# Smaller and re-timed projection pieces in a gated cross-attention and mixture-of-experts kernel, with a re-ordered start and a moved last result

## The chip, the cores and the metric

The kernel runs on one core of a Trainium2 chip. It is one launch: its inputs lie in the chip's memory, its output goes there. The metric is the device time in microseconds (us), here the median of three executions. All times and rows in this document come from those executions, from one further execution recorded by the hardware profiler, or from questions put to that record's trace.

## What is computed

Four batches of 512 tokens of width 256 attend to a context of 1601 keys of width 192, in 16 heads of 16; then a mixture of experts with a shared expert and the best two of eight follows. All of it is in float32. The reference, cut to what matters:

```python
def xattn(x, y):                       # x (4,512,256), y = ctx (4,1601,192)
    q = heads(x @ Wq + bq); k = heads(y @ Wk + bk); v = heads(y @ Wv + bv)
    attn = softmax(q @ k.T * 0.25)     # 16 heads of 16
    h = relu((attn @ v) @ W1 + b1)     # 256 -> 512
    return h @ W2 + b2                 # 512 -> 256

def moe(x):                            # 8 routed experts, 2 per token, I = 512
    probs = sigmoid(x @ Wr + rb)
    w, idx = top_k(probs, 2)
    return expert_shared(x) + sum(w[k] * expert[idx[k]](x) for k in range(2))
    # expert(x) = (silu(x @ Wg.T) * (x @ Wu.T)) @ Wd.T

x = x + tanh(g_xattn) * xattn(layernorm(x), ctx)
x = x + tanh(g_ffn) * moe(layernorm(x))
```

## The kernel before

**Groups and steps.** The 16 heads of a batch are worked on in four groups of four, so there are 16 groups over the four batches. A group has 13 steps, one for each tile of 128 keys (the last has 65). In a step TensorE makes the four scores of the next key tile (L475), ScalarE takes their exponentials (L484), TensorE adds the values of the present tile to the group's sums (L496, `add_values`), and for the softmax's shift TensorE makes scores once more for the *next* group (L416), of which VectorE takes row maxima (L427). The work of a step comes in two bursts of two scores and two maxima each. Scores have three PSUM banks, maxima three, the values' sums one, and one bank ("ms", `side()`) serves everything else. A step is written (g, k) within a batch or over all groups: group g from 0 to 15, key tile k from 0 to 12; group 4b is the first of batch b. So groups 0 to 3 are batch 0, and 12 to 15 the last batch.

**The hand-written order.** Inside the first part of the program the order on TensorE, ScalarE, VectorE and SyncE (SP, which issues DMAs) is that of the code. Work besides attention is cut into pieces and written into a list `late` of each step (`put`, `put_all`, L628 and L635): they are issued behind the step's bursts. The pieces are these:

- `make_k` (L359): a part of K for two groups: 2 matmuls of 401 columns and a ScalarE eviction into `kd`; four parts (`chunks`) make 1601 columns. `spread` (L376) then copies a group's rows out of `kd` into one of three key buffers, by four DMAs.
- `make_q` (L332): half of the Q of two groups, 2 matmuls of 256 columns and an eviction into `qd`; `spread_q` (L350) copies a group's rows by four DMAs.
- `make_v` (L387): V of one key tile, 2 matmuls of 256 columns. `make_xnT` (L305): half of the transposed layer norm, 4 transposes of 128 columns.
- `mlp_in` (L559, 2 matmuls of 256 columns, 8 pieces a batch) and `mlp_out` (L574, 4 matmuls of 128 columns, 8 pieces) for the batch before; `residual` (L589), which is VectorE work after every second `mlp_out`; then `rstd_of` (L261) and `apply` (L284) make the second layer norm, with GpSimd (Pool) taking the last of it; `route` (L594) sends its rows to memory and makes the router's logits.
- `divide`, `collect`, `normalize`: the division of the sums by the softmax's denominator, and the DMAs ahead of it.

A step with a piece that uses TensorE is put into the set `large`. A step that isn't large, is not its group's first and still has maxima to make splits `add_values` into two halves of 256 columns, one behind each burst; all others add the values in one go behind the first burst:

```python
        halves = maxima and s > 0 and s % NKT and s not in large
```

**Where the pieces stand.** While batch b is attended to, K and Q for its own second pair of groups stand in (4b, 0) to (4b, 5) (K only for b > 0; batch 0's is made at the start), and those for the first pair of the next batch in (4b+2, 0) to (4b+2, 7): K in quarters, then xnT in two, then Q in two. V of the next batch fills group 4b+3. The previous batch's `mlp_in` stand in (4b, 7) to (4b+1, 2), its `mlp_out` in (4b+1, 3) to (4b+1, 10), and `rstd_of` and `apply` in (4b+1, 11). Steps without any TensorE piece are called free steps below.

**The start.** `first_loads` (L199) issues the first DMAs. ScalarE's queue issues the one of wk, into `wk_slots`, then those of bk (two), bq, the gates and bv; SP's issues x of batch 0 in two halves, the context in four parts (two, then wq, then two), and wv. ScalarE then copies the weights of K out of `wk_slots` without their gaps (L737), K's first two parts are made (`first_k`), ScalarE and SP issue the first `spread` between them (L380, two DMAs each), ScalarE copies xnT (L303), and the first Q, the rest of K and the maxima of group 0 follow.

**The experts.** Behind attention the 4096 pairs of token and expert are sorted into tiles of 128 rows of one expert each. 35 tiles (`SURE`) are always run, four more stand in a branch that is taken only if the sorting needs them (`tc.If(n_used[0] > SURE)`, L1226); in the profiled execution it isn't taken. `run_tiles` (L1170) makes a tile's hidden layer `hT2[i]`; `give` (L1143) multiplies it by the expert's down weights, VectorE scales the result (`y`, three buffers) and Pool sends it to memory by an indirect DMA (`rows_y`). `give(SURE - 1)` stands ahead of the branch. Behind it the results are loaded (L1243), added to x (L1256) and stored, with pieces of the shared expert (`fill`, L804 and L827) between them.

Of the kernel before, what the change touches and what calls it, by code (L numbers as in the profile page):

```python
# [8 lines left out]
FP = mybir.dt.float32  # L9
# [5 lines left out]
P = 128  # L15
# [11 lines left out]
def kernel(  # L27
# [45 lines left out]
    nc = tc.nc  # L73
    B, D, M = ctxT.shape
    NT, H = x.shape
    S = NT // B
# [27 lines left out]
        xb = resid.tile([P, NTB, H], FP, name=f"xb{b}")  # L104
        xs.append(xb)

    def load_x(b, parts=1):
        n = NTB // parts
        for k in range(parts):
# [72 lines left out]
    def load_ctx(b, parts=((0, M),)):  # L182
        for o, n in parts:
            nc.sync.dma_start(
                out=ctx_t[:KC, :, o : o + n],
                in_=ctxT[b].rearrange("(c p) m -> p c m", p=KC)[:, :, o : o + n],
            )

    wk_slots = p1.tile([P, NF, S], FP, tag="hid", name="wk_slots")[:KC, :2, :]

    def without_gaps(dst, src, queue):
# [7 lines left out]
    def first_loads():  # L199

        nc.scalar.dma_start(out=wk_slots, in_=wk.rearrange("(c p) n -> p c n", p=KC))
        load_x(0, 2)
        load_ctx(0, chunks[:2])
        nc.sync.dma_start(out=wq_t, in_=wq.rearrange("(c p) n -> p c n", p=P))
        load_ctx(0, chunks[2:])
        without_gaps(bk_d, bk, nc.scalar)
        nc.scalar.dma_start(out=bq_t, in_=bq)
        nc.scalar.dma_start(out=gt, in_=gates.partition_broadcast(P))
        nc.scalar.dma_start(
            out=wv_t[KC : KC + 1, 1, :], in_=bv.rearrange("(o n) -> o n", o=1)  # L210
        )
        nc.sync.dma_start(out=wv_t[:KC], in_=wv.rearrange("(c p) n -> p c n", p=KC))

    def other_loads():
# [95 lines left out]
    def half_of(h):  # L310

        return slice(0, S) if h is None else slice(h * S // 2, (h + 1) * S // 2)
# [16 lines left out]
            )  # L329
        nc.scalar.activation(qT[i], ps, AF.Identity, bias=bq_t[:, i : i + 1])  # L330

    def make_q(b, h2, h):  # L332

        ps = side()
        n = half_of(h)
        for c in range(2):
            nc.tensor.matmul(
                ps[:, n],
                lhsT=wq_d[:, c, h2 * P : (h2 + 1) * P],
                rhs=xnT[b][:, c, n],  # L340
                start=(c == 0),
                stop=(c == 1),
            )
        if not h:
            qd[b, h2] = sp1.tile([P, S], FP, tag="qd", name=f"qd_{b}_{h2}")
        nc.scalar.activation(
            qd[b, h2][:, n], ps[:, n], AF.Identity, bias=bq_d[:, h2 : h2 + 1]
        )
# [7 lines left out]
                out=qT[i][j * HS : j * HS + HD, :], in_=qd[b, g // 2][r : r + HD, :]  # L356
            )

    def make_k(b, h2, part, ps=None):  # L359
        if part == 0:  # L360
            kd[b, h2] = sp1.tile([P, M], FP, tag="kd", bufs=2, name=f"kd_{b}_{h2}")
        o, n = chunks[part]
        ps = side() if ps is None else ps
        for c in range(2):
            nc.tensor.matmul(
                ps[:, :n],
                lhsT=wk_t[:, c, h2 * P : (h2 + 1) * P],
                rhs=ctx_t[:KC, c, o : o + n],
                start=(c == 0),
                stop=(c == 1),  # L370
            )
        nc.scalar.activation(
            kd[b, h2][:, o : o + n], ps[:, :n], AF.Identity, bias=bk_d[:, h2 : h2 + 1]
        )
# [264 lines left out]
    for b in range(B):  # L639
        i = b * G  # L640
        nb = b + 1 if b + 1 < B else None
        for g in range(G):
            if i + g:
                put(late, i + g, *((1, normalize) if i + g == NG - 1 else (0, collect)), i + g - 1)

        if b:
            put_all(i, range(NCH), [(make_k, b, 1, part) for part in range(NCH)])
            put(late, i, NCH - 1, spread, i + 2)
            put_all(i, range(2, 2 + LOTS), [(divide, b - 1, 1, t) for t in range(LOTS)])
        put_all(i, (4, 5), [(make_q, b, 1, h) for h in range(2)])  # L650
        put(late, i, 5, spread_q, i + 2)
        put(late, i + 1, 0, spread, i + 3)
        put(late, i + 1, 2, spread_q, i + 3)
        if b:
            mlp = [(mlp_in, b - 1, n % NF, n // NF) for n in range(2 * NF)]
            put_all(i, (7, 8, 9, 10, 12), mlp[: NF + 1])
            put_all(i + 1, (0, 1, 2), mlp[NF + 1 :])
            for n in range(2 * NTB):
                put(late, i + 1, 3 + n, mlp_out, b - 1, n // 2, n % 2)
                if n % 2:  # L660
                    put(late, i + 1, 4 + n, residual, b - 1, n // 2)
            put(late, i + 1, 11, rstd_of, b - 1, mv2, rstd2, nc.gpsimd)
            put(late, i + 1, 11, apply, b - 1, mv2, rstd2, nc.gpsimd)
            put_all(i + 2, (8, 9, 10, 12), [(route, b - 1, n) for n in range(4)])

        put_all(i + 2, range(2, 2 + LOTS), [(divide, b, 0, t) for t in range(LOTS)])
        if nb:
            put(late, i, 4, load_ctx, nb)
            for t in range(NTB):
                put(late, i, 6 + t, stats1, nb, t)  # L670
            put(late, i + 1, 3, rstd_of, nb, mv1, rstd1, nc.gpsimd)
            put(late, i + 1, 3, apply, nb, mv1, rstd1, nc.gpsimd)
            if not b:
                put(late, i + 1, 8, load_expert, 0, w_sh)
            put_all(i + 2, range(NCH), [(make_k, nb, 0, part) for part in range(NCH)])
            put(late, i + 2, NCH - 1, spread, i + 4)
            put_all(i + 2, (4, 5), [(make_xnT, nb, c) for c in range(2)])
            put_all(i + 2, (6, 7), [(make_q, nb, 0, h) for h in range(2)])
            put(late, i + 2, 7, spread_q, i + 4)
            put(late, i + 3, 0, spread, i + 5)  # L680
            put(late, i + 3, 2, spread_q, i + 5)
            vals = [(make_v, nb, kt) for kt in range(NKT)]
            put_all(i + 1, (12,), vals[:1])
            put_all(i + 3, [kt for kt in range(NKT) if kt != NKT - 2], vals[1:])
# [38 lines left out]
    with tc.manual_schedule(  # L723
# [12 lines left out]
        for c in range(2):  # L736
            nc.scalar.copy(  # L737
                wk_t[:, c, :].rearrange("p (h d) -> p h d", d=HD),
                wk_slots[:, c, :].rearrange("p (h d) -> p h d", d=HS)[:, :, :HD],
            )  # L740
        for t in range(NTB):
            stats1(0, t)
        rstd_of(0, mv1, rstd1, nc.vector)
# [426 lines left out]
    def run_tiles(first, end):  # L1170
        for i in range(first, end):
            own(i)
            gp = ps_g.tile([P, I], FP, tag="g", name="gp")
            half(i, gp, 0)
            up = ps_u.tile([P, I], FP, tag="u", name="up")
            half(i, up, 2)
            sg = work.tile([P, I], FP, tag="sg")
            nc.scalar.activation(sg, gp, AF.Silu)  # L1178
            hT2[i] = work.tile([P, I], FP, tag="hT2", name=f"hT2_{i}")
            nc.vector.tensor_tensor(hT2[i], sg, up, ALU.mult)  # L1180
            if i + 1 < end:
# [15 lines left out]
    with tc.manual_schedule(engines=every):  # L1197
        choose()
        fill(3)
        finding = find_places()  # L1200
        next(finding)
        fill(2)
        next(finding)
        ready = [prepare(0)]
        for _ in finding:
            pass
        fill(4)
        for part in range(NJ // PART):
# [12 lines left out]
        take(0)  # L1221
        fill(1)
        run_tiles(0, SURE)
        fill(1)
        give(SURE - 1)
    with tc.If(n_used[0] > SURE):  # L1226
        with tc.manual_schedule(engines=every):
            take(SURE)
# [4 lines left out]
    with tc.manual_schedule(  # L1233
        engines={mybir.EngineType.PE, mybir.EngineType.DVE, mybir.EngineType.Pool}
    ):
        yk = {}
        for b in range(B):
            for k in range(TOP):
# [120 lines left out]
```

## Time and profile before

| what | value |
|---|---|
| three executions | 1199.41, 1199.28, 1199.27 us |
| median | 1199.28 us |
| profiled execution, its own time | 1199.35 us |
| profiled execution, span of the record | 1197.6 us |
| mean granted clock of TensorE | 0.999 |
| maxima on VectorE, L427 | 744 times, 686 ns each |
| exponentials on ScalarE, L484 | 804 times, 594 ns each |
| DMA queue q1 (loads, spreads, stores) | 43.67 MB |
| DMA queue q0 (indirect transfers) | 8.42 MB |

The span runs from the first to the last recorded instruction; the profiled execution's own time is 1.75 us longer. By the starts of the exponentials the attention steps begin at 58.88 us with (0, 0); ahead of that lie the loads, the first K, Q and maxima, and the first V.

How to read the rows: `PE` is TensorE's matmuls and `PEld` its weight loads, which overlap them; `DVE` is VectorE, `ACT` ScalarE, `POOL` GpSimd; a name with q (`ACTq`) is the engine's sequencer, which issues DMAs and waits on semaphores. In a timeline a row gives the start, the busy time, the engine, the line of the kernel, the instruction, its output and inputs by name (`out<-in`), partitions by elements, and the count of equal neighbours; brackets at its end give the idle time ahead of it and what ended that. In a table of windows a row gives a stretch, its length, and then the busy time of PE, PEld, DVE, ACT and Pool in it with the number of their instructions, the granted clock, the DMA engines' busy share and GB/s. In a row that comes from the page's 40 slices or from the DMA view, each digit is the busy share of one slice in tenths.

### The profile page before, as it was taken

Reading aid. Unit: us, or ns where it says so; the run is one execution under the profiler, and the core shown is the slowest. Engines: PE = TensorE matmul, PEld = TensorE weight load, DVE = VectorE, ACT = ScalarE, POOL = GpSimd, SP = SyncE. Lnnn points to the kernel's source line nnn. Section 1 sums busy time; section 2 is a strip of 40 time slices with the busy share of each in tenths; the row PEclk is TensorE's granted clock in tenths of the full one; section 3 lists DMA queues with packets and bytes.
Section 4 is the critical chain, followed back from the end, with each engine's and each line's share of the span. In section 5 each row is a group of like instructions: output and inputs, shape, how many; then the busy total and the mean of one; then the engine's idle time right before and its main releaser. Section 6 shows DMA issues by size and latency. Waiting matters only on the chain. (4 is left out here: it accounts for less than half of the span.)

```text
span 1197.6 us, 21547 instructions
## 1 busy us (share of the span) xinstructions
PE 1188.0 (99%) x8454; PEld 590.5 (49%) x8454; DVE 738.1 (62%) x1394; ACT 604.6 (50%) x1112; POOL 166.0 (14%) x240
## 2 busy tenths in 40 slices
PE   9999999999999999999999999999999999999998
PEld 3433334333344343343434333343436679999995
DVE  6867767667776765676767667677604843333335
ACT  2265656555655655555556556655682233333330
POOL 2000200000022000002010000002000035555550
PEclk9999999999999999999999999999999999999999
DMA  5311110102100110121011101100009101111106
GB/s 131 107 47 26 56 24 5 28 10 60 27 2 10 37 28 1 22 49 27 2 22 32 19 10 19 28 1 28 1 7 375 58 28 41 52 44 46 46 30 215
DMA packets 37608, 54.00 MB, mean 45 GB/s; under 512 B 9339, under 2 KB 25597, under 8 KB 37506
## 3 DMA queue, kind: packets, MB, share of 16 engines
q1 hardware_dynamic: 32024, 43.67, 13.8%
q0 software_dynamic: 4656, 8.42, 2.3%
q8 instruction: 69, 1.13, 0.4%
q10 hardware_dynamic: 826, 0.50, 0.2%
q14 instruction: 33, 0.27, 0.1%
HBM read 32.88 MB, written 8.80 MB: 35 GB/s over the span
## 5 line engine op out<-in xcount | busy, mean ns | idle before, releaser
L427 DVE TENSOR_REDUCE mxs<-mx 128x1 f32<-128x512 f32 x744 | 479.9, 686 | 214.0 <-PE mx L416 207.2
L484 ACT ACTIVATE es<-sc 128x512 f32<-128x512 f32 x804 | 437.8, 594 | 328.5 <-PE mx L416 274.8
L416 PE MATMUL mx<-ks,qs 32*128 32x512 f32 (+1 forms) x1984 | 481.3, 549 | 0.2 <-DVE mxs L427 0.2
L475 PE MATMUL sc<-qA,ks 32*128 32x512 f32 x1608 | 466.1, 637 | 0.8 <-DVE qA L470 0.8
L475 PEld LDWEIGHTS sc<-qA,ks 32*128 32x128 f32 x1608 | 130.6, 179 | 215.5 <-issue 162.6
L496 PE MATMUL av<-es,vs 128*32 128x512 f32 (+3 forms) x2032 | 232.3, 527 | 0.2
L416 PEld LDWEIGHTS mx<-ks,qs 32*128 32x128 f32 x1984 | 165.3, 183 | 4.3 <-DVE mxs L427 2.4
L496 PEld LDWEIGHTS av<-es,vs 128*32 128x32 f32 (+1 forms) x2032 | 40.4, 108 | 181.3 <-issue 175.6
L269 POOL TENSOR_SCALAR var<-var 128x4 f32<-128x4 f32 x6 | 1.4, 236 | 766.4 <-DVE first L266 766.4
L1180 DVE TENSOR_TENSOR hT<-sg,up 128x512 f32<-128x512 f32 x35 | 24.1, 688 | 111.0 <-PE up L1135 107.7
L1135 PEld LDWEIGHTS gp<-xT,held 128*128 128x128 f32 x560 | 68.0, 192 | 2.2 <-ACT sg L820 0.2
L1135 PE MATMUL up<-xT,held 128*128 128x128 f32 x560 | 68.2, 275 | 0.0
L1135 PE MATMUL gp<-xT,held 128*128 128x128 f32 x560 | 68.2, 275 | 0.0
L1146 PE MATMUL y_ps<-w_all,hT 128*128 x280 | 66.2, 379 | 0.0
L1135 PEld LDWEIGHTS up<-xT,held 128*128 128x128 f32 x560 | 65.3, 192 | 0.0
L393 PE MATMUL ms<-wv_t,ctx_t 96*128 96x256 f32 (+1 forms) x208 | 58.7, 404 | 0.1
L393 PEld LDWEIGHTS ms<-wv_t,ctx_t 96*128 96x128 f32 (+1 forms) x208 | 34.5, 185 | 40.0 <-issue 31.9
L1146 PEld LDWEIGHTS y_ps<-w_all,hT 128*128 128x128 f32 x280 | 50.5, 190 | 5.5
L1178 ACT ACTIVATE sg<-gp 128x512 f32<-128x512 f32 x35 | 20.9, 597 | 61.8 <-PE gp L1135 57.5
L1126 ACT COPY held<-w_all 128x1024 f32 x39 | 40.6, 1046 | 16.0 <-issue 7.1
L1155 POOL DMA_INDIRECT rows_y<-y,dest x35 | 36.2, 1034 | 72.8 <-DVE y L1154 70.3
L1091 POOL DMA_INDIRECT xg<-rows_x,token x38 | 39.2, 1032 | 50.4 <-DVE hits L1079 39.1
(191 smaller groups left out, 954.8 us busy)
## 6 DMA issues: line engine op xcount, KB each, us to landing
ks<-kd SPq DMA_DIRECT2D x60, 100.1 KB, 3.4
w_all<-in_wgT SPq DMA_DIRECT2D x8, 512.0 KB, 10.4
w_all<-in_wuT SPq DMA_DIRECT2D x8, 512.0 KB, 10.2
w_all<-in_wdT SPq DMA_DIRECT2D x8, 512.0 KB, 10.4
w_all<-rows_y SPq DMA_DIRECT2D x8, 512.0 KB, 7.6
ctx_t<-in_ctxT SPq DMA_DIRECT2D x3, 1200.8 KB
rows_x<-xn SPq DMA_DIRECT2D x4, 512.0 KB, 3.0
qs<-qd SPq DMA_DIRECT2D x56, 32.0 KB, 2.0
```

The lines of the kernel that those rows point to most:

```text
L393: nc.tensor.matmul(ps[:n, : NH * HD], lhsT=ctx_t[r, c, o : o + n], rhs=heads[r, c, :, :HD], start=(c == 0), stop=(c == 1),)
L416: nc.tensor.matmul(ps[:, n * REST : (n + 1) * REST] if last else ps, lhsT=qT[i][slot_of(j), qb * P : (qb + 1) * P], rhs=ks[i % 3][slot_of( ...
L427: nc.vector.tensor_reduce(mxs[i][:, qb, j, c : c + 1], ps, AX.X, ALU.max)
L475: nc.tensor.matmul(ps[:n, :], lhsT=ks[i % 3][r, o : o + n], rhs=qA[i][r, :], start=True, stop=True)
L484: nc.scalar.activation(es[(i * NKT + kt) % 2, j][:n], ps[:n], AF.Exp, scale=SCALE)
L496: nc.tensor.matmul(av[i][j * HS : (j + 1) * HS, cols], lhsT=v_of(b, kt)[:n, g * HPG + j, :], rhs=es[(i * NKT + kt) % 2, j][:n, cols], star ...
L1091: nc.gpsimd.indirect_dma_start(out=xg[i % 4], out_offset=None, in_=rows_x, in_offset=bass.IndirectOffsetOnAxis(ap=token[:, i : i + 1], axi ...
L1126: (nc.scalar.copy if engine is nc.scalar else nc.vector.tensor_copy)(held[i % 2].rearrange("p c i -> p (c i)")[:, o * I : (o + 2) * I], w_ ...
L1135: nc.tensor.matmul(ps[:, f * P : (f + 1) * P], lhsT=held[i % 2][:, off + c, f * P : (f + 1) * P], rhs=xT[i][:, c, :], start=(c == 0), stop ...
L1146: nc.tensor.matmul(ps, lhsT=hT2[i][:, f * P : (f + 1) * P], rhs=w_flat[:, bass.ds(owners[i] + 4 * I + f * H, H)], start=(f == 0), stop=(f ...
L1155: ins = nc.gpsimd.indirect_dma_start(out=rows_y, out_offset=bass.IndirectOffsetOnAxis(ap=dest[:, i : i + 1], axis=0), in_=y, in_offset=Non ...
L1180: nc.vector.tensor_tensor(hT2[i], sg, up, ALU.mult)
```

## The change

It has four parts.

1. **K and Q of batch 0's successor.** K for the first pair of batch 1 is made in eighths (201 columns) instead of quarters, in (1, 0) to (1, 7) instead of (2, 0) to (2, 3); xnT goes to (1, 8) and (1, 9), and Q is made in quarters (128 columns) in (2, 4) to (2, 7). The two spreads stay where they were.
2. **The last batch.** K for its second pair is made in eighths in (12, 0) to (12, 7), with its spread behind the last; the two halves of Q go from (12, 4), (12, 5) to (12, 8), (12, 9), and their spread with them. `mlp_in` of the batch before takes (12, 10), (12, 12) and (13, 0) to (13, 5); `mlp_out` takes (13, 6) to (13, 10), (13, 12), (14, 0) and (14, 1); each `residual` follows a step behind; `rstd_of` and `apply` go from (13, 11) to (14, 2).
3. **The start.** ScalarE gets one small copy right behind the issue of wk's DMA, which brings its table load there. The first part of the context is issued between the two halves of x, and the second behind them. The DMAs of the gates and bv are issued behind the copies of K's weights.
4. **The branch.** `give(SURE - 1)` moves behind the branch, and the last sure tile's hidden layer is kept in a part of `x2T` that is free by then, instead of a rotating buffer.

Batches 1 and 2 keep their order. The diff, cut to its core:

```diff
     def first_loads():
         nc.scalar.dma_start(out=wk_slots, in_=wk.rearrange("(c p) n -> p c n", p=KC))
-        load_x(0, 2)
-        load_ctx(0, chunks[:2])
+        nc.scalar.copy(early, ident[:, :1])
+        load_x(0, 2, (0,))
+        load_ctx(0, chunks[:1])
+        load_x(0, 2, (1,))
+        load_ctx(0, chunks[1:2])
         nc.sync.dma_start(out=wq_t, in_=wq.rearrange("(c p) n -> p c n", p=P))
         load_ctx(0, chunks[2:])
         without_gaps(bk_d, bk, nc.scalar)
         nc.scalar.dma_start(out=bq_t, in_=bq)
-        nc.scalar.dma_start(out=gt, in_=gates.partition_broadcast(P))
-        nc.scalar.dma_start(
-            out=wv_t[KC : KC + 1, 1, :], in_=bv.rearrange("(o n) -> o n", o=1)
-        )
         nc.sync.dma_start(out=wv_t[:KC], in_=wv.rearrange("(c p) n -> p c n", p=KC))
...
-    def make_q(b, h2, h):
+    def make_q(b, h2, h, of=2):
-        n = half_of(h)
+        n = slice(h * S // of, (h + 1) * S // of)
...
+    eighths = [(c * (CH // 2 + 1), min(CH // 2 + 1, M - c * (CH // 2 + 1))) for c in range(2 * NCH)]
...
-    def make_k(b, h2, part, ps=None):
+    def make_k(b, h2, part, ps=None, pieces=chunks):
-        o, n = chunks[part]
+        o, n = pieces[part]
...
-        if b:
+        if nb and b:
             put_all(i, range(NCH), [(make_k, b, 1, part) for part in range(NCH)])
             put(late, i, NCH - 1, spread, i + 2)
+        elif b:
+            pieces = [(make_k, b, 1, part, None, eighths) for part in range(2 * NCH)]
+            put_all(i, range(2 * NCH), pieces)
+            put(late, i, 2 * NCH - 1, spread, i + 2)
...
-        put_all(i, (4, 5), [(make_q, b, 1, h) for h in range(2)])
-        put(late, i, 5, spread_q, i + 2)
+        q_at = (4, 5) if nb else (8, 9)
+        put_all(i, q_at, [(make_q, b, 1, h) for h in range(2)])
+        put(late, i, q_at[1], spread_q, i + 2)
...
-            mlp = [(mlp_in, b - 1, n % NF, n // NF) for n in range(2 * NF)]
-            put_all(i, (7, 8, 9, 10, 12), mlp[: NF + 1])
-            put_all(i + 1, (0, 1, 2), mlp[NF + 1 :])
+            free = [(i, kt) for kt in ((7, 8, 9, 10, 12) if nb else (10, 12))]
+            free += [(i + 1, kt) for kt in range(NKT) if kt != NKT - 2 and (kt != NKT - 1 or not nb)]
+            free += [(i + 2, kt) for kt in range(3)]
+            free = iter(free)
+            for n in range(2 * NF):
+                put(late, *next(free), mlp_in, b - 1, n % NF, n // NF)
             for n in range(2 * NTB):
-                put(late, i + 1, 3 + n, mlp_out, b - 1, n // 2, n % 2)
+                at, kt = next(free)
+                put(late, at, kt, mlp_out, b - 1, n // 2, n % 2)
                 if n % 2:
-                    put(late, i + 1, 4 + n, residual, b - 1, n // 2)
-            put(late, i + 1, 11, rstd_of, b - 1, mv2, rstd2, nc.gpsimd)
-            put(late, i + 1, 11, apply, b - 1, mv2, rstd2, nc.gpsimd)
+                    put(late, *divmod(at * NKT + kt + 1, NKT), residual, b - 1, n // 2)
+            at = (i + 1, NKT - 2) if nb else (i + 2, 2)
+            put(late, *at, rstd_of, b - 1, mv2, rstd2, nc.gpsimd)
+            put(late, *at, apply, b - 1, mv2, rstd2, nc.gpsimd)
...
-            put_all(i + 2, range(NCH), [(make_k, nb, 0, part) for part in range(NCH)])
-            put_all(i + 2, (4, 5), [(make_xnT, nb, c) for c in range(2)])
-            put_all(i + 2, (6, 7), [(make_q, nb, 0, h) for h in range(2)])
+            if b:
+                put_all(i + 2, range(NCH), [(make_k, nb, 0, part) for part in range(NCH)])
+                put_all(i + 2, (4, 5), [(make_xnT, nb, c) for c in range(2)])
+                put_all(i + 2, (6, 7), [(make_q, nb, 0, h) for h in range(2)])
+            else:
+                pieces = [(make_k, nb, 0, part, None, eighths) for part in range(2 * NCH)]
+                put_all(i + 1, range(2 * NCH), pieces)
+                put_all(i + 1, (8, 9), [(make_xnT, nb, c) for c in range(2)])
+                put_all(i + 2, (4, 5, 6, 7), [(make_q, nb, 0, h, 4) for h in range(4)])
...
                 wk_slots[:, c, :].rearrange("p (h d) -> p h d", d=HS)[:, :, :HD],
             )
+        nc.scalar.dma_start(out=gt, in_=gates.partition_broadcast(P))
+        nc.scalar.dma_start(
+            out=wv_t[KC : KC + 1, 1, :], in_=bv.rearrange("(o n) -> o n", o=1)
+        )
...
-            hT2[i] = work.tile([P, I], FP, tag="hT2", name=f"hT2_{i}")
+            if i == SURE - 1:
+                hT2[i] = x2T[:, 0, :I]
+            else:
+                hT2[i] = work.tile([P, I], FP, tag="hT2", name=f"hT2_{i}")
...
         fill(1)
-        give(SURE - 1)
     with tc.If(n_used[0] > SURE):
...
+        give(SURE - 1)
         yk = {}
```

More of the change, by code (lines that the diff above doesn't have):

```diff
@@ L105, with load_x @@
         xs.append(xb)
-    def load_x(b, parts=1):
+    def load_x(b, parts=1, which=None):
         n = NTB // parts
-        for k in range(parts):
+        for k in range(parts) if which is None else which:
             r = b * S + k * n * P
@@ L187, in load_ctx @@
             )
+    early = const.tile([P, 1], FP, name="early")
     wk_slots = p1.tile([P, NF, S], FP, tag="hid", name="wk_slots")[:KC, :2, :]
@@ L674 @@
                 put(late, i + 1, 8, load_expert, 0, w_sh)
-            put_all(i + 2, range(NCH), [(make_k, nb, 0, part) for part in range(NCH)])
+            if b:
+                put_all(i + 2, range(NCH), [(make_k, nb, 0, part) for part in range(NCH)])
[6 more added lines that the diff above has]
+                put_all(i + 2, (4, 5, 6, 7), [(make_q, nb, 0, h, 4) for h in range(4)])
             put(late, i + 2, NCH - 1, spread, i + 4)
-            put_all(i + 2, (4, 5), [(make_xnT, nb, c) for c in range(2)])
-            put_all(i + 2, (6, 7), [(make_q, nb, 0, h) for h in range(2)])
             put(late, i + 2, 7, spread_q, i + 4)
```

## The prediction

> **What bounds the kernel now.** I read the engine shares first, then cut the run into the steps of the hand-written order and priced each kind of step, then read the start and the branch near the end instruction by instruction. The page's head:
>
> ```profile
> span 1197.6 us, 21547 instructions
> ...
> PE 1188.0 (99%) x8454; PEld 590.5 (49%) x8454; DVE 738.1 (62%) x1394; ACT 604.6 (50%) x1112; POOL 166.0 (14%) x240
> ```
>
> TensorE has work queued nearly always, so what counts is how long its queue takes, stalls inside it included. I write (g,k) for the step that adds the values of key tile k of group g, and time a step from its first exponential (L484) to that of the next step. Kinds of step, in the table of windows (columns: stretch and length, busy us of each engine, granted clock, DMA share, GB/s):
>
> ```profile
> 127.05:130.62 3.57, 3.57 (x34) 1.23 (x32) 2.58 (x4) 2.17 (x5) 3.46 (x4) 1.00 0.02 5
> 161.68:166.36 4.68, 4.68 (x32) 1.46 (x36) 2.58 (x4) 2.76 (x6) 0.00 (x0) 1.00 0.00 0
> 179.44:183.43 3.99, 3.99 (x30) 1.47 (x28) 3.17 (x7) 2.65 (x5) 0.00 (x0) 1.00 0.00 0
> 223.22:227.42 4.20, 4.20 (x32) 1.46 (x36) 2.58 (x4) 2.48 (x6) 0.00 (x0) 1.00 0.00 0
> 815.55:820.39 4.84, 4.65 (x38) 1.32 (x40) 4.25 (x11) 2.17 (x5) 2.63 (x13) 1.00 0.00 0
> ```
>
> In order: a free step, 3.57; one with a quarter of K (2 matmuls of 401 columns), 4.68; with half of xnT (4 transposes), 3.99; with a V tile (2 of 256 columns), 4.20; and (13,12), which has no piece but follows the residual and rstd_of of (13,11), 4.84. The clock is full in all. K against V: 0.48 us for 290 columns more, so 1.66 ns a column; V's 512 columns are 0.85, and its step has 3.35 besides. Of that, 3.14 are two bursts of scores and maxima (1.07 each, 417.27 to 418.34 below) and one unsplit addition of values (1.00); 0.20 goes between a piece and its neighbours. The timeline of TensorE shows a floor:
>
> ```profile
> 417.27 0.69 PE L475 MATMUL sc<-qA,ks 32*128 32x512 f32 x1
> ...
> 418.34 0.66 PE L300 MATMUL ms<-ident,xn 128*128 128x128 f32 x4
> 418.93 0.69 PE L475 MATMUL sc<-qA,ks 32*128 32x512 f32 x1
> ...
> 419.14 0.69 PE L475 MATMUL sc<-qA,ks 32*128 32x512 f32 x1
> ```
>
> The transposes end at 418.93, but the second score of the next burst starts at 419.14: there are three score banks, and it waits for an exponential. So a piece that fills less than about 0.84 us between two bursts saves nothing more, and a step with a piece costs at least 3.14 + 0.84 = 3.98. Free steps escape it by splitting the addition of values over both gaps.
>
> The start, in the timeline, with the 40 slices of 0.4 us of the DMA view of 0 to 16 us:
>
> ```profile
> 6.04 1.28 ACT L737 ACT_TABLE_LOAD   x1 [6.04 <-DMA wk_slots<-in_wk]
> 7.33 0.71 ACT L737 COPY wk_t<-wk_slots 96x256 f32<-96x256 f32 x2
> ...
> 11.00 0.60 ACT L372 ACTIVATE kd<-k,bk_d 128x401 f32<-128x401 f32 x1 [0.75 <-PE k L365]
> ...
> 11.67 1.51 ACTq L380 DMA_DIRECT2D ks<-kd  x2
> ...
> 13.23 1.07 ACT L303 COPY xnT<-xnT 128x512 f32<-128x512 f32 x2 [1.63 <-issue]
> 13.87 0.30 PEld L323 LDWEIGHTS q<-xnT,wq_t 128*128 128x128 f32 x2 [0.66 <-ACT xnT L303]
> ```
> ```profile
> DMA  0000297699999999999799969899999999997610
> ```
>
> ScalarE's queue is in order: it issues two DMAs of the K spread before it copies xnT, and q, the last K part and the first maxima (17.12) follow one behind the other. From there to the first step no gap is filled by a DMA wait, so a delay here reaches the end in full. The DMA engines are full from 3.2 to 14.4 us.
>
> **The start.** Removed: nothing but the table load's place. Added: one small copy with the load ahead of it, hidden while wk is on its way. [...] Eight DMA semaphores go round, and a DMA waits until the last one on its semaphore has landed. SP now takes seven of the first eight (both halves of x, ctx in four, wq) and issues without a wait; before, wq waited 3.5 us and the third ctx part 1.1. ScalarE's take the waits: its first bk_d waits for x's first half, the second for ctx 0, bq for x's second half; then the copies of wk; gt waits for ctx 1, bv for wq; then both kd; the first spread DMA for ctx part 2, the second for wv. Behind the last one stand the xnT copies, for which q waits on TensorE, and all behind it.
>
> When these land: x's second half now goes behind ctx 0. It landed at 6.17 with 0.92 MB ahead of and in it; with 1.22 MB about 7.3. So bq is issued by 7.9, and the copies run 7.9 to 8.7, 0.6 later than now: K's weights are not sooner. wq lands around 10.7 (now 11.0), bv goes out by 11.1, kd 11.1 to 12.4. VectorE's layer norm loses 1.1 (6.17 to 7.3) and gives xn by 12.5, so it isn't last. [...] By the row there are a 7, a 6 and an 8 between 7.6 and 10.4 us to be filled, 0.36 us, and the spread's own packets, which now come before 14.4, leave some room. I take wv's last packet at 13.6 (13.1 to 14.2, now 14.4) and its semaphore 0.8 later (as x's: last packet 5.4, landing 6.2): 14.4. [...]
>
> **Batch 0, steps (1,0) to (2,7).** 18 steps. Before, by kinds: 4 x 4.68 + 2 x 3.99 + 2 x 4.20 (half of Q: 512 columns) + 10 x 3.57 = 70.8 (the trace has 71.3). After: an eighth of K has 402 columns, 0.67 + 0.20 = 0.87, just over the floor: 4.01. A quarter of Q has 256, 0.43 + 0.20 = 0.63, under it: 3.98, as for xnT; no row of that size exists, and the bounds are 3.77 (no floor) and 4.20. 8 x 4.01 + 2 x 3.99 + 4 x 3.98 + 4 x 3.57 = 70.3. The unsplit step at a group's start moves from (1,0) to (2,0), even. The evictions of eighths (8 instead of 4) lie in ScalarE's idle 0.8 us or more per step; without that cover each would be 0.4. Pool has xn of batch 1 ready at 132, before (1,8). **-0.5** (-1.0 to +0.3).
>
> **Batch 3, steps (12,0) to (14,3),** 125.8 us now. K in eighths: 8 x 4.01 - 4 x 4.68 - 4 x 3.57 = -0.9. Three MLP pieces leave (12,7) to (12,9), 3 x 0.63 = -1.9, and those at the end of the row come into (13,12), (14,0), (14,1): 4.84 + 3.10 + 4.17 = 12.1 becomes 4.45 (as (12,12)) + 2 x 4.23 (as other L578 steps) = 12.9, +0.8. That is cheap because the stall of (13,12) leaves with the residual and rstd_of; but these (1.8 us of VectorE) go to (14,2), beside a divide (0.8), where VectorE has 1.0 to spare. I charge 0.9 again, as (13,12) shows; bounds 0.3 and 1.2. The residual in (14,0): +0.3. Q's spread is issued after (12,9) and used from (12,11), one step later instead of five: its four DMAs took 4.45 us from the matmuls' end (735.1) to the last landing (739.6), the step between takes 4.13: +0.3 (0 to 0.8). SP has nothing else queued then; the K spread, four steps later, still has 16 us. Sum **-0.5** (-1.8 to +0.7).
>
> **The branch.** TensorE's work is the same, in another order. It waits at the branch for VectorE either way:
>
> ```profile
> L1226 POOLq INC_SWDGE_SEM  x1: 2364/2364/2364, 1171.5 to 1171.5; - x1
> ```
> ```profile
> 1168.67 3.72 PE L827 MATMUL op<-w_sh,hT 128*128 128x256 f32 x16 [0.64 <-DVEq L1226]
> ```
>
> Before, the last result's y precedes this; after, y waits for a semaphore that Pool adds at the end of its 2.36 us, since its buffer could have been used in the branch. Pool starts that when the previous rows_y has landed (issued 1165.38, 2.35 to land, 0.3 of waits): 1168.1 to 1170.4. y ends at 1170.9; the second shared down-piece needs y's bank and would have started at 1168.67 - 1.72 + 2 x 1.72 = 1170.4: **+0.5** (0 to 0.8). rows_y and the loads behind it come 0.4 sooner, which nobody waits for: the first add (1179.98) already follows VectorE's own work.
>
> **Sum.** +2.0 - 0.5 - 0.5 + 0.5 = +1.5 on 1199.35 (span 1197.6, 1.75 around it; the median is 1199.28): **1200.8 us**.
>
> **Rivals.** *ScalarE is held longer by wv* (the other side): place, the second L380 on ScalarE; price, one us for each us; it decides from a landing at 15.3, which makes the start +2.9. For it: the DMA row is full to 14.4 and the small packets of bk_d and bq now fall among the loads. Against: that needs the loads slower than now. 1202.2. *The start is not held*, only K's weights and the layer norm count: -0.3 there, so 1198.5; against it stands the built order. *No floor*: an eighth costs 3.81, a quarter 3.57, 16 x 0.2 + 4 x 0.41 = -4.8, 1196.0; the xnT row speaks against it, for it only that free steps of 3.57 exist.
>
> **Chances.** Forecast 0.65, wv later 0.25, start not held 0.06, no floor 0.04. A measurement can tell about 0.2% (2.4 us) from no change: faster 0.04, within 0.71, slower 0.25. The range, 1198.8 to 1202.6, takes in the start's bounds against the batches'.
>
> **What would show it.** ScalarE's xnT copies near 15.3 with a DMA wait before the second L380, and the first maxima near 19; steps of 4.0 for eighths and quarters alike; (13,12) near 4.45 and a stall after (14,2); y of the last result ending near 1170.9 on before's clock. Wrong if the xnT copies start by 13.5, or if steps with quarters take 3.8.

## The result, and the profile after

The changed kernel takes 1207.99 us (median of six executions, 1206.39 to 1210.32), the kernel before 1199.34 (six, 1198.91 to 1199.82): ratio 1.0074, interval 1.006 to 1.0088, 8.65 us slower where 1.5 were forecast. The six lie in two groups: three at 1206.4 to 1206.6 with a mean granted clock of 0.998, three at 1209.4 to 1210.3 with 0.995. The profiled one took 1209.35. The page's head:

```profile
span 1207.5 us, 21495 instructions
...
PE 1192.0 (99%) x8422; PEld 594.6 (49%) x8422; DVE 737.6 (61%) x1394; ACT 605.1 (50%) x1123; POOL 165.5 (14%) x240
...
PEclk9999999999999999999999999998999999999999
```

There are fewer instructions and more TensorE time. The 8 in the row of the granted clock (tenths of full speed, by slice) is the first sign: before, every slice was 9. Offsets of the same events against before's trace, in us, locate the loss:

| part | forecast | profiled execution |
|---|---|---|
| start, to step (0,0) | +2.0 | +5.43 |
| batch 0, to (3,0) | -0.5 | -0.45 |
| batch 3, (12,0) to (14,2) | -1.4 | -1.75 |
| (14,2) to (15,0) | +0.9 | +4.65 |
| branch, to the last down-piece | +0.5 | +1.87 |
| sum | +1.5 | +9.75 (span: +9.9) |

The start, in the timeline of the changed kernel, and then three rows of the kernel before:

```profile
5.56 1.77 ACTq L195 DMA_DIRECT2D bk_d<-in_bk  x2
...
7.71 0.36 ACTq L211 DMA_DIRECT2D bq_t<-in_bq  x1
...
8.11 0.71 ACT L757 COPY wk_t<-wk_slots 96x256 f32<-96x256 f32 x2 [5.39 <-DMA bk_d<-in_bk]
...
14.26 1.08 ACT L374 ACTIVATE kd<-k,bk_d 128x401 f32<-128x401 f32 x2 [5.44 <-DMA gt<-in_gates]
15.41 1.51 ACTq L382 DMA_DIRECT2D ks<-kd  x2
...
16.97 1.07 ACT L303 COPY xnT<-xnT 128x512 f32<-128x512 f32 x2 [1.63 <-issue]
...
17.61 2.85 PE L323 MATMUL q<-xnT,wq_t 128*128 128x512 f32 x4 [2.76 <-ACT xnT L303]
```
```profile
1.24 1.75 ACTq L194 DMA_DIRECT2D bk_d<-in_bk  x2
...
9.66 0.60 ACT L372 ACTIVATE kd<-k,bk_d 128x401 f32<-128x401 f32 x1 [1.61 <-PE k L365]
...
13.87 1.98 PE L323 MATMUL q<-xnT,wq_t 128*128 128x512 f32 x4
```

The biases go out late and the copies of wk stand behind them, as forecast. But the first eviction of K starts at 14.26, not at 11.1. The gates, which the row names, are not its input and landed 5.9 after their issue, at 14.5; bk is its input, and by the trace's semaphores its second half landed at 14.14 (at 9.29 in the kernel before). The two DMAs in L382 follow back to back with no wait for wv between them. TensorE stands idle for 2.76 us, and q then takes 2.85 for what took 1.98 before. The windows tell why (columns as before: PE, PEld, DVE, ACT, Pool, clock, DMA share, GB/s):

```profile
14.00:16.00 2.00, 0.84 (x3) 0.19 (x1) 0.00 (x0) 1.08 (x2) 0.00 (x0) 1.00 0.00 0
...
18.00:20.00 2.00, 2.00 (x4) 0.83 (x3) 0.00 (x0) 0.54 (x2) 0.00 (x0) 0.65 0.01 3
20.00:22.00 2.00, 2.00 (x4) 1.00 (x3) 0.00 (x0) 0.69 (x1) 0.00 (x0) 0.50 0.00 0
...
134.55:138.56 4.01, 4.01 (x32) 1.42 (x36) 2.58 (x4) 2.49 (x5) 4.01 (x4) 1.00 0.02 4
...
188.89:192.88 3.99, 3.99 (x30) 1.52 (x28) 3.17 (x7) 2.43 (x5) 0.00 (x0) 1.00 0.00 0
...
834.45:841.56 7.11, 6.24 (x36) 1.63 (x40) 4.91 (x13) 2.17 (x4) 5.04 (x15) 0.73 0.00 0
841.56:846.26 4.70, 4.70 (x32) 1.39 (x32) 2.91 (x5) 2.17 (x5) 2.48 (x3) 0.67 0.26 94
```

Behind the idle time TensorE runs at half its clock, from 18.6 to 22 us. The fourth and fifth rows are a step with an eighth of K and one with a quarter of Q: 4.01 and 3.99, the floor. The last two are (14,3) and (14,4): half clock again, from 837.8 to 844.6. What stands ahead of that, in the timeline:

```profile
833.78 0.48 DVE L593 SCALAR_TENSOR_TENSOR xb<-y,tg,xb 128x256 f32<-128x256 f32 x1
...
835.62 0.55 DVE L527 RECIPROCAL oS<-oS 128x64 f32<-128x64 f32 x1
...
836.35 1.88 DVE L429 TENSOR_REDUCE mxs<-mx 128x1 f32<-128x512 f32 x3
...
837.09 1.42 PE L418 MATMUL mx<-ks,qs 32*128 32x512 f32 x2 [0.87 <-DVE mxs L429]
```

VectorE does the residual, rstd_of and a divide between two bursts of maxima, 2.4 us of work; the three banks of maxima are full, and TensorE waits 0.87 for one.

My theory after this: the change makes three waits of TensorE (bk at the start, VectorE after (14,2), y at the branch), and each can be followed by a stretch of half clock that costs more. The rivals: the start is held by the ring of DMA semaphores, as I forecast; the half clock comes by chance; the moved result costs what it costs alone.

### The profile page after: what moved, and what is told of

It reads as the page before. It is cut to its first block, busy times and chain, and to the rows that moved or that the text cites. A ratio compares the mean times of both kernels' runs of the same rounds, so it can differ in the third digit from the quotient of the medians.

```text
span 1207.5 us, 21495 instructions
## 1 busy us (share of the span) xinstructions
PE 1192.0 (99%) x8422; PEld 594.6 (49%) x8422; DVE 737.6 (61%) x1394; ACT 605.1 (50%) x1123; POOL 165.5 (14%) x240
## 4 chain that ended last, share of the span: by engine, by line
PE 95%; DVE 2%; DMA 1%; ACT 0%; issue 0%; ACTq 0%; DVEq 0%
PE sc L477 33%; PE av L498 18%; PE gp L1159 5%; PE up L1159 5%; PE mx L418 5%; PE y_ps L1170 5%; PE ms L395 5%; PE ms L367 4%; PE ms L580 2%; PE ms L567 2%; PE gp L828 2%; PE op L851 2%; PE up L828 2%; PE ms L337 1%; PE sc L418 1%; DMA xg<-rows_x,token 1%
## 5 line engine op out<-in xcount | busy, mean ns | idle before, releaser
L367 PE MATMUL ms<-ctx_t,wk_t 96*128 96x401 f32 (+3 forms) x144 | 47.4, 451 | 0.0
## 6 DMA issues: line engine op xcount, KB each, us to landing
w_all<-in_wuT SPq DMA_DIRECT2D x8, 512.0 KB, 10.3
```

The lines of the kernel that those rows point to most:

```text
L367: nc.tensor.matmul(ps[:, :n], lhsT=wk_t[:, c, h2 * P : (h2 + 1) * P], rhs=ctx_t[:KC, c, o : o + n], start=(c == 0), stop=(c == 1),)
```

## The experiments

Each kernel was timed beside the kernel before, which had 1199.39 for the first four, 1199.18 for the next four, 1199.35 for the three after them and for the late lists together, and 1199.28 for the two shifted ones. These four sets ran on four chips.

**Biases first** (the changed kernel with one edit):

```diff
         nc.scalar.dma_start(out=wk_slots, in_=...)
+        without_gaps(bk_d, bk, nc.scalar)
+        nc.scalar.dma_start(out=bq_t, in_=bq)
         nc.scalar.copy(early, ident[:, :1])
...
-        without_gaps(bk_d, bk, nc.scalar)
-        nc.scalar.dma_start(out=bq_t, in_=bq)
```

> The changed kernel, with one change: the DMAs of bk and bq are issued right behind wk's, ahead of x and the context, so that they wait for no semaphore. Theory A (the first K eviction waited for bk, which was issued at 5.56 and 6.77 us and came in behind the loads at 14.17): evictions near 10 and 11.5, xnT copies near 13.3 instead of 16.97, no fall of the clock at 18 us, first maxima near 17; the start loses all of its 5.4 us, so 1201.1 where the clock holds later, 1204.5 where it falls in step (14,3). Theory B (ScalarE stands behind wv and the context in the ring of semaphores, as I forecast): wv lands no sooner, xnT copies stay at 15 or later, gain at most 2 us.

Measured: 1207.34 (1205.43 to 1207.58). Its timeline:

```profile
5.74 0.71 ACT L757 COPY wk_t<-wk_slots 96x256 f32<-96x256 f32 x2 [0.61 <-DMA wk_slots<-in_wk]
...
9.70 0.60 ACT L374 ACTIVATE kd<-k,bk_d 128x401 f32<-128x401 f32 x1 [3.25 <-DMA bk_d<-in_bk]
...
13.23 1.07 ACT L303 COPY xnT<-xnT 128x512 f32<-128x512 f32 x2 [1.85 <-PE xnT L300]
```

The eviction comes 4.6 us sooner, xnT 3.7, and the half clock at the start is gone: theory A. That the ring of semaphores holds ScalarE behind wv falls. Step (0,0) is 0.85 behind before instead of 5.43; the 0.85 is x's second half, behind the context's first part, and the layer norm with it. The time expected was missed all the same, since in this profile the clock fell at 833 and at 1175 us, in the waits after (14,2) and at the branch, 1.7 us each.

**The start's wait filled:**

```diff
         first_k(2)
+        for n in range(3):
+            nc.tensor.matmul(warm, lhsT=ks[2][:, :P], rhs=ks[2][:, :S], start=True, stop=True)
```

> The changed kernel, with three more warming matmuls of 512 columns (2.6 us at full clock) on TensorE behind K's third part, where TensorE stood idle from 14.85 to 17.61 us. Theory A1 (1.7 of the start's 5.4 us come from the clock, 0.5 from 18.6 to 22 us, which fell because TensorE had stood idle): clock 1.00 throughout, q's matmuls 2.0 instead of 2.85 us, steps begin 1.7 us sooner, 1204.8 where the clock holds later. Theory A2 (the half clock has another cause, or the lost time is waiting alone): the same 64.3 us for the first step, or later by what the added matmuls overrun.

Measured: 1204.79 (1203.66 to 1206.95). Its profile, by windows and in the timeline:

```profile
18.00:20.00 2.00, 1.87 (x5) 0.91 (x6) 0.00 (x0) 1.06 (x3) 0.00 (x0) 1.00 0.17 37
```
```profile
18.13 1.98 PE L323 MATMUL q<-xnT,wq_t 128*128 128x512 f32 x4 [0.51 <-ACT xnT L303]
```

The clock is 1.00 from 14 to 24 us and falls nowhere else before TensorE's work ends; q's matmuls take 1.98; step (0,0) comes 1.2 us sooner (xnT itself was 0.5 later here). The wait of 3.7 is still there: so wait and clock are two costs. That the second follows from TensorE's idleness rests on this one profile against the five others with the late start and the wait unfilled, which all fell there (the table at the end of this section).

**VectorE given room**, and **the last result back ahead of the branch** (each in the changed kernel; with the second, the last hidden layer is back in the rotating buffer too):

```diff
-            at = (i + 1, NKT - 2) if nb else (i + 2, 2)
+            at = (i + 1, NKT - 2) if nb else (i + 2, 3)
-        put_all(i + 2, range(2, 2 + LOTS), [(divide, b, 0, t) for t in range(LOTS)])
+        o = 2 if nb else 4
+        put_all(i + 2, range(o, o + LOTS), [(divide, b, 0, t) for t in range(LOTS)])
```
```diff
         run_tiles(0, SURE)
         fill(1)
+        give(SURE - 1)
     with tc.If(n_used[0] > SURE):
...
-        give(SURE - 1)
         yk = {}
```

> The changed kernel, with the divides of the last batch's first pair two steps later, (14,4) to (14,11), and rstd_of and apply at (14,3), so that VectorE has room for the last residual. Theory C (VectorE's 2.4 us of residual, rstd_of and divide in (14,2) stalled TensorE for 0.87 us, and the clock fell to 0.5 for some 7 us behind it, in half of the executions): no stall over 0.3 us there, clock 1.00 in all executions, all within 0.5 us of each other, about 1.2 us below the faster of the changed kernel's two groups (1206.5): 1205.3. Theory D (the clock falls by chance, whatever the stall): two groups 3.4 us apart remain.

> The changed kernel, with the last sure result computed ahead of the branch again. Theory E (behind the branch it costs 1.9 us: VectorE's y waits for a semaphore that Pool adds only when the previous rows_y has landed, and the next down-piece of the shared expert waits for y's bank): 1.9 less than the changed kernel, 1204.6 or 1208.0 by the clock in (14,3). Theory F (my forecast: 0.5): 1206.0 or 1209.4.

Measured: 1205.31 (1203.78 to 1206.92) with room. Its step (14,3):

```profile
834.86:838.75 3.89, 3.89 (x36) 1.39 (x40) 3.32 (x9) 2.17 (x5) 0.47 (x3) 1.00 0.00 0
```

The stall is gone, at full clock, but against theory C's forecast the executions aren't within 0.5 us of each other: the start's and the branch's waits are still there, and this profile lost 1.7 at the start. 1206.89 (1204.89 to 1209.51) with the old place; its executions lie at 1204.9 to 1205.3, 1206.9 and 1209.4 to 1209.5, so the medians don't tell theory E from F. The trace speaks for E: 0.57 above before at the branch instead of 1.87, so 1.3 of the 1.9. But 0.57 is left where the code is that of before: a cost I had not seen.

**One part alone, in the kernel before:** batch 0 and batch 3 are the change's own hunks, batch 3 with VectorE's room; the start is new; the last has all three.

```diff
         nc.scalar.dma_start(out=wk_slots, in_=...)
+        without_gaps(bk_d, bk, nc.scalar)
+        nc.scalar.dma_start(out=bq_t, in_=bq)
+        nc.scalar.copy(early, ident[:, :1])
         load_x(0, 2)
         load_ctx(0, chunks[:2])
...
-        without_gaps(bk_d, bk, nc.scalar)
-        nc.scalar.dma_start(out=bq_t, in_=bq)
-        nc.scalar.dma_start(out=gt, in_=gates.partition_broadcast(P))
...
                 wk_slots[:, c, :].rearrange("p (h d) -> p h d", d=HS)[:, :, :HD],
             )
+        nc.scalar.dma_start(out=gt, in_=gates.partition_broadcast(P))
...
```

> The kernel before, with the change's first part alone (K of batch 1 in eighths in group 1, xnT behind it, Q in quarters). In the profile of the changed kernel the steps up to (3,0) gained 0.45 us by it. Theory G (that gain is real and nothing behind it moves): 0.45 less than before, 1198.9. Theory H (the first part brings a stall and with it a fall of the clock in some executions): single executions 1.7 us higher, or a loss.

> The kernel before, with the change's second part alone, and with the divides of the last pair two steps later and rstd_of and apply at (14,3), as in the run in which VectorE had room. There the steps of the last batch gained 1.6 us. Theory G: 1.6 less than before, 1197.8. Theory H (the gain comes back as a stall or a half clock among the experts): 1199.4 or more.

> The kernel before, with ScalarE's table load ahead and bk and bq issued right behind wk's DMA, the gates and bv behind the copies of K's weights, and SP's order of x and context as before. The run with the biases first lost 0.85 us at the start, since x's second half landed at 7.82 us and the layer norm was ready later. Theory A (with x's order kept, K's weights come 1.3 us sooner and the spread's DMAs and xnT with them): xnT copies near 12.4 instead of 13.23, 0.8 less than before, 1198.6. Rival (the ring of DMA semaphores or the full DMA engines hold K's spread where it was): within 0.3 of before.

> The three runs sent with this one together: first part, second part with the divides later, the start with the biases first and x's order kept; the last sure result stays ahead of the branch. Theory G (the parts don't touch one another): the sum, 0.45 + 1.6 + 0.8 = 2.9 less than before, 1196.5, and no half clock. Theory H (one of them brings a stall with a fall of the clock): 1.7 or 3.4 us above that in some executions.

Measured: batch 0 1198.86, ratio 0.9995 (0.9987 to 1.0004), the trace gains 0.45 from (0,0) to (3,0) and ends 0.35 ahead of before, a gain that the ratio can't tell from none. Batch 3 1197.40, ratio 0.9985 (0.9978 to 0.9992): theory G, and all 21 executions within 0.6 us. The start 1199.38, ratio 1.0003 (0.9995 to 1.0012): xnT at 12.83 and step (0,0) 0.4 ahead in the trace, but nothing in the medians, so inconclusive. All three 1198.08 (1197.73 to 1198.66) where 1196.5 was expected: no half clock, but the trace loses 0.55 at the branch again, and the start brings nothing.

**The other parts as they were made, alone** (the hunks of the change's diff for the start, for batch 3 and for the last result, each in the kernel before):

> The kernel before, with the change's third part alone, as it was made (early copy, first context part between the halves of x, gates and bv later). Theory A: xnT copies near 17 us as in the changed kernel, since bk is issued late: 3.7 above before, and 1.7 more where the clock falls to half for one stretch of 3.4 us at 18 us, as in three of four profiles: 1204.6 in most executions, 1202.9 in the others. Theory B (the start costs that much only together with the other parts): under 1201.5.

> The kernel before, with the change's second part alone, as it was made (divides from (14,2), rstd_of and apply at (14,2)). Against the same with the divides later (1197.4) the traces showed 1.6 us for the stall after (14,2), and none, one or two stretches of half clock of 3.4 us behind it. Theory C: executions in groups at 1199.0, 1200.7 and 1202.4, their granted clock 0.999, 0.998 and 0.996. Theory D (the half clock there comes from the lost time at the start, not from this stall): all within 0.5 us of 1199.0.

> The kernel before, with the change's fourth part alone (last sure result behind the branch). Theory E: 1.4 to 1.9 above before by the traces, so 1200.6 to 1201.1, as rows_y takes 3.2 to 4.2 us to land instead of the 2.35 of my forecast and y ends 11 to 12 us after the last tile's first weights instead of 10.2; 1.7 more where the clock falls in the wait. Theory F (my forecast of 0.5): 1199.7.

Measured: the start 1208.27 (1207.32 to 1208.92), worse than expected: in its profile the wait is the same 3.7, but the half clock lasts two stretches (17 to 24 us, 3.4 lost), and one more, 1.7, follows (13,12), whose stall of 0.19 the kernel before has too. Of 102 executions of the kernel before, 20 lie at 1200.4 to 1201.2, some 1.5 above the others. Of 56 executions of the kernels with batch 3 and VectorE's room and no late start (batch 3 alone, all three, and the late lists below, unshifted and shifted), in which (13,12) has no such stall, none lies that far above the others of its kernel. So that stall is where they come from, as far as counts can tell; none of the 20 was profiled.

Batch 3: four executions at 1199.0 to 1199.6 (clock 1.0), six at 1200.5 to 1201.0, one at 1202.6: the steps of theory C, 1.7 us apart, with no late start behind them. The stall alone, in the window of (14,3) of its profile:

```profile
829.89:835.31 5.42, 4.55 (x36) 1.38 (x40) 5.09 (x13) 2.17 (x4) 3.35 (x14) 1.00 0.00 0
```

Here TensorE idles for the same 0.87 us, and the clock stays at 1.00. Against 3.85 before the step costs 1.57.

The moved result: 1199.86 (1199.42 to 1201.41), ratio 1.0005 (0.9996 to 1.0014), the trace +0.44: theory F, my forecast. So the changed kernel's 1.87 had another term. TensorE's branch instruction and the wait of Pool for rows_y (min/median/max ns), first in the changed kernel, then in this one:

```profile
L1253 POOLq EVENT_SEMAPHORE  x4: 17/43/3336, 1173.5 to 1177.0; - x4
...
L1253 PEldq COMPARE_BRANCH  x1: 3727/3727/3727, 1170.4 to 1170.4; - x1
```
```profile
L1229 POOLq EVENT_SEMAPHORE  x4: 17/43/1902, 1165.7 to 1167.8; - x4
...
L1229 PEldq COMPARE_BRANCH  x1: 476/476/476, 1162.5 to 1162.5; - x1
```

The branch takes 3.7 instead of 0.5, and rows_y lands 1.4 later. Queue q8 of the changed kernel's profile holds 69 packets of kind instruction, 16 KB each, some 15 us apart among the experts. Up to the branch 179 to 336 recorded instructions of TensorE, 256 on average, lie between the starts of two (201 to 300, 256, in the kernel before), so I take them for fetches of its code. In the changed kernel none begins in the 14 us ahead of the branch, then one 1.0 us behind the branch's start and another 4.5 us behind it, while rows_y is on its way. Here one begins 3.0 us ahead of the branch and the next 1.2 us behind its start; in the kernel before, whose branch takes 0.47, 5.9 ahead and 1.2 behind.

**The late lists together, and the code shifted.** The shift, in that kernel and in the changed one, adds 24 instructions of TensorE and leaves the columns as they were but for two:

```diff
-        for n in range(4):
-            nc.tensor.matmul(warm, lhsT=ks[0][:, :P], rhs=ks[0][:, :S], ...)
+        for n in range(10):
+            nc.tensor.matmul(warm[:, :205], lhsT=ks[0][:, :P], rhs=ks[0][:, :205], ...)
```

> The kernel before, with the first part as it was made and the second with the divides later, the start and the branch as before. Theory G (their gains add): 0.3 and 1.8 below before, 1197.1, faster than both kernels; no half clock. Rival (the first part's gain is lost again by batch 3): 1197.4 or more.

> The kernel with the first part and the mended second part (1197.9 on its chip, branch 0.43 above before), with the warming matmuls at the start cut into ten of 205 columns instead of four of 512, the same columns with 24 more instructions of TensorE, all in time that it waits anyway. Theory I (where the 16 KB pieces of TensorE's code end decides: with 17069 and 17081 instructions ahead of the branch the fetch falls into it and it takes 2.8 to 3.7 us, with 17085, 17117 and 17133 it takes 0.47): with 17093 the branch takes 0.47, no fetch 1 us behind its start, the shared expert's second down-piece 7.88 us after the last tile's first weights instead of 8.3, 0.43 less. Theory J (the branch is slow because of the parts' own work): 3 us as before, no gain.

> The changed kernel, with the same 24 more instructions of TensorE at the start. Theory I (its branch cost 1.9 us instead of 0.5 because the fetch of TensorE's code delays the landing of rows_y to 3.6 us, and Pool's semaphore and y with it): branch 0.47, rows_y lands in 2.2 us as with that part alone, y ends 10.1 us after the last tile's first weights, 1.4 less than the changed kernel: 1205.1 where the clock falls once, 1208.5 where it falls three times. Theory J: no difference.

Measured: together 1197.93 (1197.77 to 1198.44), above the rival's 1197.4: both gains are in the trace (1.86 at (15,0)), and 0.43 goes at the branch. Shifted 1197.33 (1197.05 to 1197.66), ratio 0.9982 (0.9973 to 0.9991), 1.86 ahead to the end. TensorE's branch, unshifted and shifted:

```profile
L1247 PEldq COMPARE_BRANCH  x1: 3087/3087/3087, 1163.9 to 1163.9; - x1
```
```profile
L1247 PEldq COMPARE_BRANCH  x1: 468/468/468, 1163.7 to 1163.7; - x1
```

Unshifted, no fetch begins in the 17 us ahead of the branch; shifted, one begins 3.1 us ahead of it. (Another still begins 1.2 us behind, where I had expected none.) All sixteen profiles agree: in eight, 17046 to 17082 instructions of TensorE are recorded ahead of the branch, and it takes 2.6 to 3.8; in the other eight, 17096 to 17144, and it takes 0.47 to 0.48. (The expectations count otherwise.) So in these sixteen the branch's time goes with its place in the code: theory I.

The changed kernel, shifted, has 1206.22 (1203.49 to 1208.51). That its branch would take 0.47 was missed: it takes 2.62, for with the shift only 17070 are recorded ahead of it. But nobody waits for that; rows_y lands 1.1 sooner, y ends at 10.3 us (10.1 expected), and the branch costs 0.76 instead of 1.87. Its start, in this profile, is 0.7 later.

The time that each profile lost to half clock, summed from windows of 1 us as (1 - granted clock), by where it fell:

| kernel | start | after (13,12) or (14,2) | branch | span less these |
|---|---|---|---|---|
| changed | 1.70 | 3.42 | - | 1202.4 |
| biases first | - | 1.71 | 1.70 | 1200.2 |
| wait filled | - | - | - | 1202.7 |
| VectorE's room | 1.71 | - | - | 1201.7 |
| result ahead again | 1.70 | - | - | 1201.4 |
| start alone, as made | 3.42 | 1.71 | - | 1201.6 |
| changed, shifted | 1.70 | - | - | 1202.3 |

Every other profile lost nothing; the fall at the very end of each, when TensorE's matmuls are over, is left out. The changed kernel's two groups of executions differ by 3.3, the cost of two stretches.

The clock's records in the traces show one thing more. In all sixteen profiles every change of the clock lies a whole number of 3.41 us behind the clock's first record, and that record lies at 4.4 to 7.6 us of the span, elsewhere in each. In the changed kernel the record is at 4.94, and 18.59, 22.00, 837.79 and 844.62 lie 4, 5, 244 and 246 times 3.413 us behind it; in the kernel before the record is at 4.83. So the same stall lies elsewhere on this grid in each profile. Six profiles have the stall after (14,2). In the two that fell there (the changed kernel, biases first) TensorE was busy for 0.75 of the grid's stretch ahead of the fall; in the four that didn't, for 0.78 or more of each stretch, in two of them because the grid cuts the stall in two. This fits one stall with several outcomes, but the busy share alone is no rule: behind 0.94 the clock fell ((13,12) in the start alone, as made), and behind 0.51 it didn't (at the branch, with VectorE's room).

## Why the prediction was wrong, point by point

- **The start: the step that failed.** "kd 11.1 to 12.4" took the bias for landed once it was issued. I had found that bk waits for x and the context in the ring of semaphores, and priced who stands behind its issue, but not when it arrives. Issued at 5.56 and 6.77 instead of 1.24 and 2.43, its two pieces of 0.5 KB were in at 14.14 instead of 9.29, and K's first eviction stood for them until 14.26. From the second issue to the landing that is 7.4 us, and 6.9 before: the time that I left out is about the same in both orders, and the kernel before hides it by the early issue. The sum's +2.0, xnT at 15.25 behind an estimated landing of wv at 14.4, is a term that no run shows: in the changed kernel's trace wv was in at 13.90, 2.2 us ahead of the spread's DMA that shares its semaphore, and the wait is one of 3.74 for bk, as the biases issued first show. wv, on which the first rival was built too, held nothing.
- **The half clock: a term that was missing.** No row of before has it in its profile. It added 1.7 at the start and 0, 1.7 or 3.4 after (14,2). The profiled execution missed the forecast by 8.25: the longer wait for bk and the half clock at the start are 3.4 of it, the half clock after (14,2) up to 3.4 more; the rest is mainly the stall and the branch, below. The falls, to 0.50 for one stretch of 3.4 us or two, came behind 2.76 us and 0.87 us of idle time, and behind 0.19 in one profile. At the 1.7 of a stretch I would have charged 1.7 to 5.1.
- **Batch 0:** right, -0.45 to (3,0), and -0.65 to the end of the forecast's 18 steps, against -0.5. Eighths take 4.01 to 4.02 and quarters 3.99, both as worked out, but for the eighths in (1,0), 4.41, and (1,7), 3.99, and the quarter in (2,4), 3.79. The rival without a floor falls.
- **Batch 3:** right to (14,2), -1.75 against -1.4. The stall of rstd_of went to (14,2) as I said; there it was mis-sized, 1.57 against 0.9 and outside its bounds of 0.3 to 1.2, for a divide and the residual stand in the same gap.
- **The branch:** mechanism and size right for the part alone, 0.44 against 0.5. In the whole change 1.87, with a fetch 1.0 us behind the branch's start and the next one 4.5 us behind it, beside rows_y; with 24 more instructions of TensorE ahead, 0.76. In the five profiles of the moved result with a fetch while rows_y is on its way it lands in 2.5 to 4.2 us, in the one without in 2.2. That the fetch makes it late is argued from their times alone; how, no run shows.
- **Open:** why the clock fell behind 0.87 us of idle time in two profiles and not in four, and why a fall lasts one stretch or two; why half a kilobyte takes 7 us to land.

The best version of all is the kernel before with the late lists, VectorE's room and the shift: 1197.33, 1.95 below the kernel before on the same chip.

## What to carry to other kernels

When DMAs are put in another order, follow each small operand to its landing, not only to its issue: here half a kilobyte landed some 7 us behind its issue in either order, and only the early issue hid it. Price every new wait of TensorE twice, for its length and for the half clock that may follow (here 1.7 us a stretch), and take executions that differ by a fixed step as a sign of the second. Where a branch takes 3 us more with unchanged code, shift it by some instructions before explaining it otherwise: here it took 3.09, and 0.47 with 24 instructions put ahead of it.

## What the runs showed of the hardware that was not expected

- TensorE's granted clock fell to 0.50 for 3.4 us at a time, 1.7 us lost each, behind idle times of 2.76 and 0.87 us (once 0.19); in time that was filled with matmuls of no use it didn't, in the one profile of that. Its changes lay whole numbers of 3.41 us behind its first record, which lay elsewhere in each profile (4.83 us in the kernel before's, 4.94 in the changed one's).
- Packets of 16 KB of kind instruction came once for some 256 recorded instructions of TensorE up to the branch. The branch took 2.6 to 3.8 us where one began 0.0 to 1.0 us behind its start and none in the 13 us ahead (3.73 in the changed kernel, with one 1.0 behind), and 0.47 to 0.48 where one began 3.0 to 6.1 us ahead (0.47 in the kernel before, 5.9 ahead).
- An indirect DMA of one row per partition landed 2.2 to 4.2 us after its issue at the same place of the program, and bk's second DMA of 0.5 KB 6.9 us (in the kernel before) and 7.4 us (in the changed one) after its issue.
